# An attention pair with four layer norms on one core: scale and shift of norm 1 moved into W1 and b1, norms 1 and 3 moved to ScalarE, order laid anew

## The chip, the core and the metric

The kernel runs on one core of one Trainium2 chip. Five engines work side by side, each with its own queue in program order: TensorE (PE; its weight loads are shown as PEld), VectorE (DVE), ScalarE (ACT), GpSimd (POOL) and SyncE (SP), which here only issues DMAs. The metric is the device time of one execution in microseconds.

## The reference

32 graphs of 512 nodes with 256 features pass through two attention layers, each with its own adjacency mask, and through four layer norms:

```python
# layer 0
x  = x0 + attention(x0, Wqkv, allowed) @ Wo.T + bo
x  = layernorm(x) * ln1_g + ln1_b                     # norm 1
ff = relu(x @ W1.T + b1) @ W2.T + b2
x  = layernorm(x + ff) * ln2_g + ln2_b                # norm 2
x  = layernorm(x0 + x)                                # norm 3
# layer 1
x  = layernorm(x + attention(x, Wq, Wk, Wv, adj) @ Wo.T + bo)   # norm 4
```

8 heads of 32, W1 from 256 to 1024; everything is float32. `allowed` is adj or its transpose or the diagonal.

## The kernel before

**Tiling.** A graph's 512 nodes are 4 row blocks of 128 partitions (NQ = 4); the 256 features are 2 blocks (ND = 2). Transposed activations (xT, qT, kT) have features on partitions.

**Stages of a graph.** They are small methods of class Graph, each of which issues a few instructions:
- `scores(layer, k)`: for a group of 4 heads and a key block (k = 0 to 7) 4 products with 32 rows of the array each, into psS (four PSUM banks, one buffer), and one exp of ScalarE into p (L340, L344). `masked(layer, k)`: VectorE multiplies p by the mask (L349).
- `product(k)`: 4 products with 32 columns of the array each into psA (L357); products 3 and 7 are followed by a copy to cT on ScalarE (L367). `sums` adds p over keys with a matrix of ones (L397); `pair` adds two p by a GpSimd DMA (L372), `fold` on VectorE (L376), so that `sums` runs once for a head group. `divide` transposes, inverts and multiplies into cT on VectorE (L409 to L416).
- `project` multiplies cT by Wo (psO). `out0`, `out1`, `out2` add the residual on VectorE and take statistics (y L444, st L425, mv L426); `root(n, a, b)` makes 1/sqrt(variance + eps) of the row blocks a to b on GpSimd in two instructions (L431, L432).
- `norm1`, `norm2` call `affine`: two VectorE instructions for each row block (L439, L440). Norm 2 puts the block of x, to which ln2_b has been added, in the place of the shift, so that it adds the residual for norm 3 in the same step. `norm3` is one VectorE instruction (L513). `norm4` is one ScalarE activation (L527), with the bias from `offset` (-mean/std, VectorE, L522).
- `transpose` turns x1 or x2 with TensorE and copies it to xT on ScalarE. `hidden(h, f)` multiplies by W1 and applies relu with b1 on ScalarE (psH L476, hT L484); `mlp` multiplies by W2 (psF L497); `query_key`, `value` are the other projections.
- For later graphs the first transpose is done by DMA: `flip` and `sort` (SP queue) and `join` (two ScalarE copies, L286). `load`, `again` load x twice (x and x1); `cast` and `entries` bring the adjacency, `masks` (VectorE) makes the two masks from it.
- `residual`, `residual1`, `residual2` add rows to x1, x, x1 and x2 by GpSimd DMAs that accumulate (`add_row`, L169). `once` and `once1` (bias rows bov from bv and Wo, TensorE psB L163 and VectorE) do something for graph 0 alone.

**PSUM.** psS takes four banks, psA one, and three buffers in turn (`ps_d`) hold all other results, so that a late reader of one of them holds up the third allocation after it.

**Order.** The order within each engine's queue is written out by hand in three lists of calls: `opening(a, b, c, d)` starts the first graphs, `period(a, b, c, d, e)` is repeated 29 times, and `closing(a, b, c)` ends the last ones. In a period, a to e are five successive graphs: c passes through layer 0's attention in the first half, b through the second half of its MLP and layer 1, a through its last projection and norm 4, d through its first projections. A period begins with c.scores(0, 0). Every engine works through its own calls of the list in order; waits between engines come from the data. Ahead of the opening the SP queue issues the loads: x of graph 0, Wqkv and its biases, the adjacency of graph 0 once it has been cast, Wo and bo of layer 0, x of graph 1, then all other weights in the order of their declaration, layer 1's Wo and bo last.

The general path for extreme inputs at the end of the kernel is not taken in these runs.

Of the kernel before, what the change touches and what calls it, by code (L numbers as in the profile page):

```python
# [9 lines left out]
F32 = mybir.dt.float32  # L10
# [17 lines left out]
def kernel(ctx: ExitStack, tc: tile.TileContext, t: dict, out: bass.AP):  # L28
# [77 lines left out]
    g1, be1 = spread("L0_gnn_ln1_g"), spread("L0_gnn_ln1_b")  # L106
    g2, be2 = spread("L0_gnn_ln2_g"), spread("L0_gnn_ln2_b")
# [11 lines left out]
    bov = [const.tile([P, D], F32, name=f"bov_{layer}") for layer in range(2)]  # L119

# [29 lines left out]
    def plain(pools: ExitStack):  # L150
# [16 lines left out]

        def add_row(dst, row):
            nc.gpsimd.dma_start(out=dst, in_=row[:, None, :].to_broadcast([P, NQ, D]), accum_op=ALU.add)  # L169
# [7 lines left out]
        class Graph:  # L177


            def __init__(self, b):  # L180
                self.b = b
                self.mv, self.rs, self.pf, self.total = {}, {}, {}, {}
# [45 lines left out]
            def once(self):  # L228

                if self.b == 0:  # L230
                    value_bias(0)

# [231 lines left out]
            def norm1(self, i):  # L464
                self.affine(self.x1[:, i, :], self.y.pop(i), g1, be1, 1, i)
# [20 lines left out]
            def residual1(self):  # L486
                add_row(self.x1, b2)
                self.tile("x2", [NQ, D])
# [22 lines left out]
            def norm3(self, i):  # L511
                mean, rs = self.mean(3, i), self.rs[3][:, i, :]
                nc.vector.tensor_scalar(self.x2[:, i, :], self.y.pop(i), mean, rs, ALU.subtract, ALU.mult)  # L513
# [4 lines left out]
            def offset(self, a, b):  # L518

                if a == 0:  # L520
                    self.ms = small.tile([P, NQ, 1], F32, tag="ms", name=f"ms_{self.b}", bufs=2)
                nc.vector.scalar_tensor_tensor(  # L522
                    self.ms[:, a:b, :], self.mv[4][:, a:b, 0:1], -1.0, self.rs[4][:, a:b, :], ALU.mult, ALU.mult
                )

            def norm4(self, i):
                nc.scalar.activation(  # L527
                    self.x2[:, i, :], self.y.pop(i), AF.Identity, bias=self.ms[:, i, :], scale=self.rs[4][:, i, :]
                )
# [7 lines left out]
        def period(a, b, c, d, e):  # L537
# [3 lines left out]
            c.scores(0, 0)  # L541
            a.fold(3, 6, 7)
            b.hidden(1, 0)
            b.hidden(1, 2)
            c.scores(0, 1)
            c.masked(0, 0)
            b.hidden(1, 4)
            b.hidden(1, 6)
            c.masked(0, 1)
            a.fold(3, 3, 4)  # L550
            c.once()
            c.scores(0, 2)
            c.masked(0, 2)
            b.mlp(3)
            b.out2(3)
            a.sums(3, 1, first=True, last=True)
            a.product(7)
            c.scores(0, 3)
            c.product(0)
            b.mlp(2)  # L560
            c.residual()
            a.divide(1)
            b.root(2, 3, 4)
            a.project(1, 0)
            c.scores(0, 4)
            b.transpose(b.x2, 0)
            b.norm2(3)
            c.masked(0, 3)
            c.pair(0)
            b.out2(2)  # L570
            b.root(3, 3, 4)
            b.root(2, 2, 3)
            b.norm3(3)
            a.out1(0)
            a.project(1, 1)
            b.norm2(2)
            c.scores(0, 5)
            c.product(1)
            b.root(3, 2, 3)
            c.product(2)  # L580
            c.product(3)
            a.out1(1)
            c.masked(0, 4)
            b.norm3(2)
            c.scores(0, 7)
            c.masked(0, 5)
            b.transpose(b.x2, 1)
            b.query_key(1, 1, 0, 0)
            c.product(4)
            a.out1(3)  # L590
            a.out1(2)
            c.pair(2)
            a.root(4, 0, 2)
            c.pair(4)
            c.scores(0, 6)
            c.masked(0, 7)
            a.offset(0, 2)
            b.query_key(1, 0, 0, 0)
            c.masked(0, 6)
            c.fold(2, 2, 0)  # L600
            b.query_key(1, 1, 0, 1)
            a.norm4(0)
            a.norm4(1)
            b.query_key(1, 0, 0, 1)
# [4 lines left out]
            c.product(5)  # L609
            c.product(6)  # L610
            a.root(4, 2, 4)
            a.offset(2, 4)
            c.product(7)
            c.sums(2, 0, first=True, last=True)
            b.scores(1, 2)
            b.query_key(1, 0, 1)
            d.entries()
            c.fold(3, 3, 4)
            c.divide(0)
            d.load()  # L620
            d.flip(0, 0)
            d.sort(0, 0)
            d.again()
            d.flip(0, 1)
            c.sums(3, 1, first=True, last=True)
            b.masked(1, 2)
            b.scores(1, 1)
            c.divide(1)
            e.cast()
            b.residual2()  # L630
            b.value(1, 0)
            b.masked(1, 0)
            a.norm4(3)
            a.norm4(2)
            b.value(1, 1)
            c.once1()
            b.masked(1, 1)
            b.scores(1, 5)
            c.project(0, 0)
            c.project(0, 1)  # L640
            b.scores(1, 3)
            c.out0(0)
            c.out0(1)
            c.root(1, 0, 2)
            c.norm1(0)
            c.norm1(1)
            b.product(0)
            b.product(1)
            b.product(2)
            d.join(0, 0)  # L650
            c.out0(3)
            c.out0(2)
            b.scores(1, 7)
            d.sort(0, 1)
            c.transpose(c.x1, 0)
            a.store()
            d.value(0, 0)
            b.scores(1, 6)
# [750 lines left out]
```

## Time and profile before

| What | Value |
|---|---|
| median of 3 runs | 3093.13 us (3093.06 to 3094.09) |
| span of the profiled execution | 3093.4 us |
| instructions in it | 44239 |
| one of the middle periods | 94.8 us |
| DMA | 406.5 MB, mean 131 GB/s |
| mean granted TensorE clock | 0.996 |

A busy share is the part of the span in which an engine has an instruction running. The ends of matmuls are modelled, so starts are safer to read than durations. In a row of instructions, what stands in square brackets is the idle time of the engine before it, and who ended it. A row of a group has the busy time in us, the mean of one in ns, and after the second bar the idle time ahead of its instructions. The 40 digits are slices of 77 us, in tenths.

### The profile page before, as it was taken

What the parts mean: (1) busy time and instruction counts of PE and PEld (TensorE: products, weight loads), DVE (VectorE), ACT (ScalarE), POOL (GpSimd) and SP (SyncE); (2) the same over time, 40 slices, a digit from 0 to 9 for tenths busy, and PEclk for the clock granted to TensorE, in tenths of its full rate; (3) what the DMA queues carried; (4) which work ended last, traced back from release to release, by engine and by line L of the source; (5) the groups of instructions that cost most, each with busy time, mean ns of one, the idle gap of its engine ahead of it and who ended that gap; (6) DMA issues with size and microseconds to landing.
All of it is one profiled execution on the core that took longest, in us unless ns stands there. A gap on an engine that the chain in (4) does not pass through costs nothing. (4 is left out here: it accounts for less than half of the span.)

```text
span 3093.4 us, 44239 instructions
## 1 busy us (share of the span) xinstructions
PE 3053.5 (99%) x17218; PEld 1729.8 (56%) x17218; DVE 2647.5 (86%) x3458; ACT 1707.7 (55%) x1983; POOL 1039.0 (34%) x1254
## 2 busy tenths in 40 slices
PE   6999999999999999999999999999999999999998
PEld 2656555555555555555655555555556555555554
DVE  4798898888898888988888988889888889888887
ACT  4455655555565556655555655556555655555554
POOL 1232334332343323333333333233333334332332
PEclk8999999999999999999999999999999999999999
DMA  8676776666676666776676766668666777666542
GB/s 191 134 135 118 140 144 139 123 130 130 137 151 123 133 125 135 147 139 126 123 136 137 147 120 133 123 137 154 131 132 115 141 143 140 124 129 126 116 89 63
DMA packets 341064, 406.54 MB, mean 131 GB/s; under 512 B 149616, under 2 KB 315632, under 8 KB 316144
## 3 DMA queue, kind: packets, MB, share of 16 engines
q0 software_dynamic: 95824, 282.09, 50.8%
q1 hardware_dynamic: 245024, 121.56, 15.9%
q8 instruction: 137, 2.24, 0.3%
q14 instruction: 79, 0.65, 0.1%
HBM read 89.01 MB, written 33.55 MB: 40 GB/s over the span
## 5 line engine op out<-in xcount | busy, mean ns | idle before, releaser
L344 ACT ACTIVATE p<-psS 128x2048 f32<-128x2048 f32 x512 | 962.3, 1880 | 652.7 <-PE psS L340 647.1
L349 DVE TENSOR_TENSOR p<-p,m 128x2048 f32<-128x2048 f32 x512 | 1155.1, 2278 | 30.6 <-ACT p L344 30.6
L431 POOL TENSOR_SCALAR rs<-mv 128x2 f32<-128x2 f32 (+1 forms) x320 | 321.7, 1005 | 936.0 <-DVE mv L426 934.0
L340 PE MATMUL psS<-qT,kT 32*128 32x512 f32 x4096 | 585.6, 641 | 7.9 <-ACT p L344 6.0
L357 PE MATMUL psA<-p,v 128*32 128x512 f32 x4096 | 491.9, 598 | 0.7 <-ACT cT L367 0.7
L497 PE MATMUL psF<-w_L_gnn_W,hT 128*128 128x256 f32 x2048 | 469.0, 382 | 0.0
L476 PE MATMUL psH<-xT,w_L_gnn_W 128*128 128x256 f32 x2048 | 467.4, 384 | 0.0
L497 PEld LDWEIGHTS psF<-w_L_gnn_W,hT 128*128 128x128 f32 x2048 | 383.7, 190 | 124.9 <-issue 77.7
L476 PEld LDWEIGHTS psH<-xT,w_L_gnn_W 128*128 128x128 f32 x2048 | 381.4, 190 | 118.3 <-issue 44.8
L376 DVE TENSOR_TENSOR p<-p,p 128x2048 f32<-128x2048 f32 x189 | 429.0, 2285 | 2.2 <-DMA p<-p 1.9
L340 PEld LDWEIGHTS psS<-qT,kT 32*128 32x128 f32 x4096 | 160.3, 183 | 305.4 <-issue 114.4
L432 POOL TENSOR_TENSOR rs<-rs,neg_half 128x2 f32<-128x2 f32 (+1 forms) x320 | 304.2, 951 | 26.8
L357 PEld LDWEIGHTS psA<-p,v 128*32 128x32 f32 x4096 | 110.0, 109 | 315.6 <-issue 234.5
L484 ACT ACTIVATE hT<-psH,c_L_gnn_b 128x256 f32<-128x256 f32 x512 | 215.2, 472 | 122.9 <-PE psH L476 119.6
L412 POOL TENSOR_TENSOR total<-total,sT 128x16 f32<-128x16 f32 x128 | 28.5, 223 | 731.2 <-DVE sT L409 731.2
L327 PE MATMUL psQK_None<-xT,w_L_gnn_Wqkv 128*128 128x512 f32 x512 | 239.1, 600 | 4.2 <-DMA w_L_gnn_Wqkv<-in_L_gnn_Wqkv_dram 2.4
L456 PE MATMUL psO<-w_L_gnn_Wo,cT 128*128 128x256 f32 x1024 | 241.1, 383 | 0.9 <-DVE cT L416 0.9
L372 POOL DMA_DIRECT2D p<-p x189 | 186.9, 991 | 142.4 <-PE psA L357 109.3
L367 ACT COPY cT<-psA 128x512 f32<-128x512 f32 x128 | 75.0, 586 | 278.5 <-PE psA L357 278.5
L444 DVE TENSOR_TENSOR y<-psF,x 128x256 f32<-128x256 f32 x128 | 53.7, 420 | 196.1 <-PE psF L497 189.6
L456 PEld LDWEIGHTS psO<-w_L_gnn_Wo,cT 128*128 128x128 f32 x1024 | 189.2, 190 | 51.9 <-DVE cT L416 22.2
L425 DVE BATCH_NORM_STATS2 st<-y 128x6 f32<-128x256 f32 x384 | 164.2, 428 | 13.1
(68 smaller groups left out, 2936.3 us busy)
## 6 DMA issues: line engine op xcount, KB each, us to landing
p<-p POOLq DMA_DIRECT2D x189, 1024.0 KB, 7.6
x<-in_x_dram SPq DMA_DIRECT2D x64, 512.0 KB, 5.2
x<-bov POOLq DMA_DIRECT2D x64, 512.0 KB, 9.1
code<-in_adj_dram POOLq DMA_DIRECT2D x32, 512.0 KB, 6.7
m<-code SPq DMA_DIRECT2D x32, 512.0 KB, 5.6
x<-s_L_gnn_ln_b POOLq DMA_DIRECT2D x32, 512.0 KB, 10.4
x<-s_L_gnn_b POOLq DMA_DIRECT2D x32, 512.0 KB, 5.4
out_dram<-x SPq DMA_DIRECT2D x32, 512.0 KB, 9.4
```

The lines of the kernel that those rows point to most:

```text
L327: nc.tensor.matmul(ps, w[:, i, c * P : (c + 1) * P], self.xT[:, i, at], start=(i == 0), stop=(i == ND - 1))
L340: nc.tensor.matmul(s[:, j, :], self.kT[at, hg, kc * P : (kc + 1) * P], self.qT[at, hg, :], start=True, stop=True)
L344: nc.scalar.activation(p, s, AF.Exp, scale=SCALE)
L349: nc.vector.tensor_tensor(p, p, m[:, k % NQ, None, :].to_broadcast([P, HPC, N]), ALU.mult)
L357: nc.tensor.matmul(self.acc[hg][j * HD : (j + 1) * HD, :], self.v[:, kc, h * HD : (h + 1) * HD], self.p[k][:, j, :], start=(kc == 0), stop ...
L376: nc.vector.tensor_tensor(self.p[dst], self.p[a], self.p[b], ALU.add)
L431: nc.gpsimd.tensor_scalar(rs, self.mv[n][:, a:b, 1:2], EPS, None, ALU.add)
L432: nc.gpsimd.tensor_tensor(rs, rs, neg_half[:, a:b, None], ALU.pow)
L456: nc.tensor.matmul(ps[:, j, :], self.cT[:, k, at], wo[layer][:, k, :], start=(k == 0), stop=(k == ND - 1))
L476: nc.tensor.matmul(ps[:, j, :], w1[:, c, at], self.xT[:, c, h * 2 * P : (h + 1) * 2 * P], start=(c == 0), stop=(c == ND - 1),)
L484: nc.scalar.activation(self.hT[h][:, f + j, :], ps[:, j, :], AF.Relu, bias=b1[:, f + j : f + j + 1])
L497: nc.tensor.matmul(ps, self.hT[h][:, f, j * P : (j + 1) * P], w2[:, f, :], start=(f == 0), stop=(f == NF - 1))
```

## The change

1. Norm 1 writes (y - mean)/std without scale and shift; `fold_norm1`, once for graph 0, multiplies W1's rows by ln1_g in place and adds W1 times ln1_b to b1, so that `hidden` is unchanged. For the residual, `residual1` multiplies x1 by ln1_g on VectorE (after the transposes have read it) and then adds the row ln1_b + b2 (row12) by the same GpSimd DMA as before.
2. Norms 1 and 3 are applied by ScalarE as norm 4 was (`shifted`), with a bias from `offset` for each.
3. The three lists are new. For norms 1 and 3 they have five more `offset` calls in a period. The load section is the same, with two more columns (ln1_g, ln1_b) among the later weights.

```diff
+    g1_c, be1_c = column("L0_gnn_ln1_g"), column("L0_gnn_ln1_b")
...
+    row12 = const.tile([P, D], F32, name="row12")
...
+        def fold_norm1():
+            ps = ps_d.tile([P, NF], F32, tag="d", name="psW_0")
+            for f in range(NF):
+                for c in range(ND):
+                    nc.tensor.matmul(
+                        ps[:, f : f + 1],
+                        w1[:, c, f * P : (f + 1) * P],
+                        be1_c[:, c : c + 1],
+                        start=(c == 0),
+                        stop=(c == ND - 1),
+                    )
+            nc.vector.tensor_tensor(b1, b1, ps, ALU.add)
+            for c in range(ND):
+                nc.vector.tensor_scalar(w1[:, c, :], w1[:, c, :], g1_c[:, c : c + 1], None, ALU.mult)
+            nc.vector.tensor_tensor(row12, be1, b2, ALU.add)
...
+            def once2(self):
+                if self.b == 0:
+                    fold_norm1()
...
             def norm1(self, i):
-                self.affine(self.x1[:, i, :], self.y.pop(i), g1, be1, 1, i)
+
+                self.shifted(1, self.x1, i)
...
             def residual1(self):
-                add_row(self.x1, b2)
+                nc.vector.tensor_tensor(self.x1, self.x1, g1[:, None, :].to_broadcast([P, NQ, D]), ALU.mult)
+                add_row(self.x1, row12)
                 self.tile("x2", [NQ, D])
...
             def norm3(self, i):
-                mean, rs = self.mean(3, i), self.rs[3][:, i, :]
-                nc.vector.tensor_scalar(self.x2[:, i, :], self.y.pop(i), mean, rs, ALU.subtract, ALU.mult)
+                self.shifted(3, self.x2, i)
...
+            def shifted(self, n, dst, i):
+                bias, scale = self.ms[n][:, i, :], self.rs[n][:, i, :]
+                nc.scalar.activation(dst[:, i, :], self.y.pop(i), AF.Identity, bias=bias, scale=scale)
```

The new list of a period, several calls to a line (`sums` without its flags):

```
c.scores(0, 0); b.hidden(1, 0); b.hidden(1, 4); a.fold(3, 6, 7); c.once(); c.scores(0, 1); b.hidden(1, 2);
b.hidden(1, 6); c.masked(0, 0); a.fold(3, 3, 4); c.masked(0, 1); a.sums(3, 1); a.product(7); c.scores(0, 3);
e.cast(); a.divide(1); c.residual(); c.masked(0, 3); b.mlp(3); b.out2(3); b.root(2, 3, 4); b.norm2(3);
c.scores(0, 4); b.mlp(2); c.masked(0, 4); c.scores(0, 2); c.product(0); b.out2(2); a.project(1, 0);
b.root(3, 3, 4); b.root(2, 2, 3); b.offset(3, 3, 4); c.masked(0, 2); c.once2(); c.scores(0, 6); b.norm2(2);
b.transpose(b.x2, 0); c.pair(0); b.root(3, 2, 3); a.out1(0); b.offset(3, 2, 3); a.project(1, 1); a.out1(1);
c.scores(0, 5); a.out1(3); c.masked(0, 5); c.product(1); a.out1(2); b.norm3(3); b.norm3(2); c.product(2);
c.product(3); c.scores(0, 7); c.product(4); c.product(5); b.transpose(b.x2, 1); b.query_key(1, 0, 0, 0);
b.query_key(1, 1, 0, 0); b.query_key(1, 0, 0, 1); c.masked(0, 6); a.root(4, 0, 2); c.pair(2);
a.offset(4, 0, 2); c.masked(0, 7); c.pair(4); c.fold(2, 2, 0); b.query_key(1, 1, 1); b.scores(1, 0);
c.fold(3, 6, 7); a.norm4(0); c.fold(3, 3, 4); a.root(4, 2, 4); c.product(6); c.sums(2, 0); c.product(7);
c.divide(0); b.scores(1, 1); b.query_key(1, 1, 0, 1); b.value(1, 0); c.sums(3, 1); c.divide(1); b.masked(1, 1);
a.norm4(1); b.scores(1, 3); b.query_key(1, 0, 1); c.project(0, 0); b.scores(1, 2); c.project(0, 1); c.out0(0);
c.out0(1); a.offset(4, 2, 4); b.residual2(); c.root(1, 0, 2); c.offset(1, 0, 2); b.masked(1, 0); c.norm1(1);
c.norm1(0); b.value(1, 1); b.masked(1, 2); a.norm4(3); c.transpose(c.x1, 0); b.scores(1, 4); a.norm4(2);
b.product(0); d.again(); d.flip(0, 0); c.out0(3); b.pair(0); d.load(); d.sort(0, 0); c.out0(2); d.entries();
d.flip(0, 1); b.masked(1, 3); b.product(1); b.product(2); d.sort(0, 1); a.store(); d.join(0, 0);
b.scores(1, 7); c.root(1, 2, 4); b.pair(2); c.offset(1, 2, 4); c.once1(); c.norm1(3); b.masked(1, 4);
c.hidden(0, 0); c.norm1(2); c.hidden(0, 2); c.hidden(0, 4); b.scores(1, 6); c.transpose(c.x1, 1);
c.hidden(0, 6); b.scores(1, 5); d.join(0, 1); d.value(0, 0); c.mlp(0); b.masked(1, 7); d.masks();
c.residual1(); d.query_key(0, 1, 0); c.mlp(1); b.masked(1, 6); b.masked(1, 5); b.fold(2, 2, 0); c.out2(0);
c.out2(1); d.query_key(0, 0, 0); d.query_key(0, 1, 1); d.query_key(0, 0, 1); d.value(0, 1); c.root(2, 0, 2);
b.product(3); b.sums(2, 0); b.product(4); b.pair(4); c.norm2(0); c.norm2(1); b.divide(0); c.root(3, 0, 2);
c.offset(3, 0, 2); b.product(5); b.product(6); c.norm3(1); c.norm3(0);
```

The new opening up to graph 0's first transpose of x1:

```
a.flip(0, 0); a.join(0, 0); a.join(0, 1); a.once(); a.query_key(0, 0, 0); a.query_key(0, 1, 0); a.value(0, 0);
a.masks(); a.scores(0, 0); a.query_key(0, 1, 1); a.masked(0, 0); a.scores(0, 3); a.value(0, 1); a.sort(0, 0);
a.scores(0, 1); a.query_key(0, 0, 1); a.scores(0, 2); a.masked(0, 1); a.masked(0, 2); a.masked(0, 3);
a.product(0); a.scores(0, 4); a.product(1); a.masked(0, 4); a.product(2); a.scores(0, 5); a.masked(0, 5);
a.product(3); a.scores(0, 6); a.pair(0); a.pair(2); a.flip(0, 1); b.flip(0, 0); a.product(4); a.pair(4);
b.sort(0, 0); a.masked(0, 6); b.cast(); b.flip(0, 1); a.fold(2, 2, 0); a.scores(0, 7); b.sort(0, 1);
a.product(5); b.join(0, 0); a.masked(0, 7); b.join(0, 1); b.value(0, 0); a.sort(0, 1); a.product(6);
a.product(7); a.sums(2, 0); a.fold(3, 6, 7); a.fold(3, 3, 4); b.entries(); a.residual(); b.residual();
a.divide(0); a.sums(3, 1); b.query_key(0, 0, 0); a.divide(1); b.query_key(0, 0, 1); a.once2();
b.query_key(0, 1, 0); a.project(0, 0); b.scores(0, 0); a.out0(0); a.out0(1); a.root(1, 0, 2);
a.offset(1, 0, 2); b.query_key(0, 1, 1); a.norm1(1); a.norm1(0); a.project(0, 1); a.out0(3); a.out0(2);
b.masks(); a.root(1, 2, 4); c.cast(); b.scores(0, 5); b.masked(0, 0); a.offset(1, 2, 4); a.transpose(a.x1, 0);
...
```

The new closing from c.mlp(0) to the middle of the last attention:

```
...
c.mlp(0); c.mlp(1); b.fold(2, 2, 0); b.masked(1, 5); b.masked(1, 6); c.hidden(1, 0); b.fold(3, 6, 7);
c.out2(0); c.out2(1); b.pair(4); c.root(2, 0, 2); c.norm2(0); b.fold(3, 3, 4); c.norm2(1); c.hidden(1, 4);
c.hidden(1, 6); c.hidden(1, 2); b.sums(2, 0); c.mlp(2); b.divide(0); c.root(3, 0, 2); c.out2(2);
c.offset(3, 0, 2); c.root(2, 2, 3); c.mlp(3); c.norm3(0); c.norm3(1); c.norm2(2); c.out2(3); c.root(2, 3, 4);
c.root(3, 2, 3); c.norm2(3); c.offset(3, 2, 3); c.root(3, 3, 4); c.once1(); b.product(5); b.product(6);
c.transpose(c.x2, 0); c.offset(3, 3, 4); b.product(7); c.norm3(2); c.norm3(3); c.query_key(1, 1, 0, 0);
b.sums(3, 1); b.divide(1); c.transpose(c.x2, 1); c.query_key(1, 0, 0, 0); c.query_key(1, 0, 0, 1);
c.query_key(1, 1, 0, 1); c.scores(1, 0); c.query_key(1, 1, 1); c.scores(1, 1); b.project(1, 0); c.scores(1, 3);
...
```

## The prediction

> **What bounds the kernel now.** I read the busy table, then TensorE's own timeline, because a busy share says nothing about slack, then the opening, where the only long idle stretches lie.
>
> Busy table and 40 slices of the page:
> ```profile
> PE 3053.5 (99%) x17218; PEld 1729.8 (56%) x17218; DVE 2647.5 (86%) x3458; ACT 1707.7 (55%) x1983; POOL 1039.0 (34%) x1254
> ...
> PE   6999999999999999999999999999999999999998
> ...
> PEclk8999999999999999999999999999999999999999
> ```
> TensorE idles in the first slice, somewhat in the last, and nowhere between. VectorE, which the change relieves, has 14% to spare.
>
> TensorE's timeline in a middle period (start, duration, what):
> ```profile
> 1500.94 3.62 PE L497 MATMUL psF<-w_L_gnn_W,hT 128*128 128x256 f32 x16
> 1504.40 1.88 PE L327 MATMUL psQK_None<-xT,w_L_gnn_Wqkv 128*128 128x512 f32 x4
> ...
> 1511.43 2.78 PE L357 MATMUL psA<-p,v 128*32 128x512 f32 x24
> 1514.14 1.14 PE L340 MATMUL psS<-qT,kT 32*128 32x512 f32 x8
> 1515.21 3.72 PE L476 MATMUL psH<-xT,w_L_gnn_W 128*128 128x256 f32 x16
> 1518.87 1.14 PE L340 MATMUL psS<-qT,kT 32*128 32x512 f32 x8
> ```
> Read starts, not durations: each group begins when the one before has run through. Sixteen full-array ("wide") matmuls of 256 columns take 3.46 us with wide neighbours (1500.94 to 1504.40: 0.216 each), but 3.66 between two score groups. So entering and leaving a wide run costs 0.20. A score group takes 1.07 everywhere. Three products take 2.71: 3 x 0.858 plus 0.14 for entering and leaving a column run (products, sums). Nothing else appears: the middle is a fixed sequence of matmuls without waits.
>
> From these prices a period is: 16 score groups x 1.071 = 17.14; 20 products and sums x 0.858 = 17.16; 256 wide units (hidden 64, mlp 64, query_key 64, project 32, value 32; each fp32 product is two records) x 0.2158 = 55.24; 16 transposes x 0.109 = 1.74; 13 wide runs x 0.198 = 2.57; 8 column runs x 0.138 = 1.10; less 0.048 for each of 4 wide runs that begin with a transpose (0.19). Sum 94.77. Measured: the period that opens at 1514.14 ends at 1608.93, 94.79. TensorE sets the pace, and only fewer runs or fewer waits at the two ends can shorten the program.
>
> The opening (all engines):
> ```profile
> 15.03 0.50 SPq L1190 DMA_DIRECT2D w_L_gnn_Wo<-in_L_gnn_Wo_dram  x1
> ...
> 16.53 1.14 PE L340 MATMUL psS<-qT,kT 32*128 32x512 f32 x8 [0.78 <-ACT kT L330]
> ...
> 45.72 2.04 PE L163 MATMUL psB<-w_L_gnn_Wo,c_L_gnn_bv 128*128 128x256 f32 x4 [10.51 <-DMA w_L_gnn_Wo<-in_L_gnn_Wo_dram]
> ...
> 49.97 0.76 ACT L286 COPY xT<-kT 128x512 uint16<-128x512 uint16 x1 [16.95 <-DMA kT<-v]
> ...
> 53.81 2.09 PE L340 MATMUL psS<-qT,kT 32*128 32x512 f32 x8 [6.04 <-ACT p L344]
> ```
> once1() (the bias row of layer 1) stands in TensorE's queue before its weights are there, and graph 1's join() stands in ScalarE's queue before its DMAs are there, with the next exp behind it: 10.5 and 6.0 us of TensorE lost. The first period starts at 186.9; the opening's matmuls at the prices above sum to 151.1, so about 36 us are lost there. The closing (from 2937.4) loses 3.5 before the last matmul, and 10 after it.
>
> **What the skill says.** "Perfetto Trace Analysis", opening note: matmul busy time is a bad measure, as matmuls are pipelined. Hence the starts above. "TensorEngine Tiling (Array Packing)", Key Properties: a change of tiling mode drains TensorE; the trace agrees and prices it (3.46 against 3.66). "SBUF — State Buffer", Who interferes with whom: a VectorE instruction with two SBUF inputs blocks a GpSimd one that reads SBUF. The trace agrees: root()'s first half is 0.36 us free, 2.15 beside a mask product:
> ```profile
> 1574.11 0.36 POOL L431 TENSOR_SCALAR rs<-mv 128x2 f32<-128x2 f32 x1 [5.47 <-DVE mv L426]
> ...
> 1578.93 2.15 POOL L431 TENSOR_SCALAR rs<-mv 128x2 f32<-128x2 f32 x1 [2.76 <-DVE mv L426]
> ```
> "TensorE: Matmul & The Clock Gate", What's actually happening: after idling, the array runs at half clock for some microseconds. The trace agrees: eight matmuls at 9.11 take 7.4 us, eight later ones 3.43.
>
> **Part by part.** Durations are means of the groups by shape.
> ```profile
> L439 DVE SCALAR_TENSOR_TENSOR cent<-y,mv,s_L_gnn_ln_g 128x256 f32<-128x256 f32 x256 | 119.3, 466 | 2.5
> ...
> L440 DVE SCALAR_TENSOR_TENSOR x<-cent,rs,s_L_gnn_ln_b 128x256 f32<-128x256 f32 x128 | 62.0, 485 | 35.9 <-POOL rs L432 30.4
> ...
> L513 DVE TENSOR_SCALAR x<-z,mv,rs 128x256 f32<-128x256 f32 x128 | 48.9, 404 | 36.8 <-POOL rs L432 36.8
> ...
> L527 ACT ACTIVATE x<-y,ms,rs 128x256 f32<-128x256 f32 x128 | 70.2, 600 | 9.5 <-DVE ms L522 9.5
> ```
> *VectorE* loses per graph 4 x (0.466 + 0.485) for norm 1 and 4 x 0.404 for norm 3 = 5.4 us. It gains five offsets x 0.15 and one multiplication of x1 by g1, 1024 wide: between 0.69 (cT, 512 wide) and 2.28 (p, 2048), 1.22. Net -3.4 per graph, -110 in all: 86% becomes 82%. *ScalarE* gains 8 x 0.55 = 4.4 per graph, 55% to 60%. Both lie beside a full TensorE: worth nothing by themselves.
>
> *The period's order.* Counting runs in the new list: wide runs 13 (hidden pair, hidden pair, mlp 3, mlp 2, project 0, transpose and project 1, transpose and query_keys, query_key and value, query_key and project, project and value and transpose, three hiddens, transpose and hidden, the long one from d.value(0, 0)), column runs 8. Same counts, but c.transpose(c.x1, 0) no longer begins a run: +0.048. Floor 94.82, x29 periods = +1.4 us.
>
> *Waits that the order adds.* (a) Norm 1's chain is longer and its window shorter. From the end of c.project(0, 0): two out0 2.04, their last mv starts at 2.05; 1.48 from there to the instruction that waits for root (1573.83 to 1575.31); offset 0.15 and hand-over 0.05; two activations, 0.50 and 0.57; to TensorE about 0.05: 4.8. TensorE fills that with scores(1, 2) 1.07, project(0, 1) 1.83 and value(1, 1) 1.73 = 4.63 before c.transpose(c.x1, 0). Wait 0.2 per period, bounds 0 and 0.35. Behind it queue all wide matmuls. Before, b.product(0..2) and another score group lay in that gap. (b) c.fold(3, 3, 4) waits for pair(4). Pairs are 1 MB POOL DMAs: two issued at 1544.32 and 1548.70 landed 7.2 and 8.4 later, so 5.6 apart. Now product(4) follows product(3) after one score group: pair(2) at about 31.5 of the period lands at 38.6, pair(4) at 44.2. Then VectorE has fold 2.20, divide(0) 2.5, divide(1) 2.6: 51.5, against c.project(0, 0) due at 51.3. Bounds 0 and 0.35; I take 0.1, since a pair issued close behind may land sooner. (c) offset stands in VectorE's queue behind root; with masks following it, VectorE idles 1 us where root was blocked, but the two places (before b.masked(1, 0), b.masked(1, 4)) leave the mask products in time by my sums (S(1, 5) due at 71.86, its psum free at about 71.7). 0. Together 0.3 x 29 = +8.7.
>
> *residual1*: the multiplication precedes the POOL DMA of row12. The product ends at about 75, landing takes 5.4 (median of the b2 row), so 81; out2(0), behind three long VectorE instructions, comes at 81.5. 0. The SP queue has d.again and d.flip first and entries() later; flip waits for c.product(7) (43.5), sort's DMAs land near 54, join is due at 62. 0.
>
> *The opening.* a.once() now stands before the first query_key, and its Wo lands at 19.6 (issued 15.03). First scores: 19.7 + 1.8 (four psB) + 6 (eight at half clock, then full) + value 1.8 = 29 instead of 16.5: +12.5. Against that once1 is late and join stands behind scores(0, 7): -16.6 and some clock warm-up. Eight scores at 3.13 (exp-bound, as 16.53, 19.68, 22.81 before) end at 52; then waits for join (2.6) and fold(3, 3, 4) (3). fold_norm1 on TensorE: 16 products of one column, two passes, 32 records, between 0.109 (a transpose) and 0.216 each: 3.5 to 6.9, I take 6.1 (weight load 0.19). Its VectorE part (two scalings of w1, bias, row12: 3 us) hides beside the next query_key. Laying both lists side by side up to the first norm 1: about +3.3, bounds -3 and +7.
>
> *The closing*: wide runs 20 to 25 = +1.0 and transposes -0.1; a norm 3 chain of 6 us in a window of 5.5 before c.transpose(c.x2, 1): +0.5. Sum +1.4, bounds -1 and +5.
>
> Sum against the profiled span, 3093.4: 3093.4 + 1.4 + 8.7 + 3.3 + 1.4 = 3108.2. The other runs shown, 3093.06 to 3094.09, lie around that span.
>
> **Rivals.**
> *Floor*: neither chain binds, 3093.4 + 1.4 + 3.3 + 1.4 = 3099.5. For it: the margins are 0.1 to 0.2 us, my error.
> *Opening pays* (the other side): fold_norm1 runs at 0.11 per record (-2.6) and join and fold find their DMAs landed (-5.6), no chain binds: 3091. It decides at the first graph's scores(0, 7): if product(5) to sums(3, 1) run without a gap, it holds; with the closing's 3.5 us of waits also gone, 3086 or less. Against: SP's load queue still ends at 41.5.
> *A new wait per period of 1 us or more*: VectorE's stand behind a blocked root() reaches exp and so a score group, or join() meets DMAs that start later. 29 x 1 on top: 3137. For it: root at 2.15 and more beside mask products; against: 15 us of VectorE's period are free.
>
> **Numbers.** Both chains (one at least): 0.54, 3108, own range 3101 to 3118. Floor 0.16. Opening pays 0.16. New wait 0.14. The range 3089 to 3129 leaves out half of the last and the end of the third. No change (within 0.2%, about what a measurement of this kernel can tell) is 3086.9 to 3099.3: half of *opening pays*, near half of *floor*, a little of the first: 0.19; faster 0.11 (half of *opening pays*, some of the closing); slower 0.70.
>
> **What would show it.** Right: period starts 95.1 apart, a wait of psT for ScalarE's x1 and of psO for cT in the list of waits, first psS near 29. Wrong: periods of 94.8 (no chain binds), a first psS before 25, or 32 psW records under 4 us.

## The result: slower, and by more than forecast

| | before | after |
|---|---|---|
| median of the runs, us | 3093.55 (4 runs, 3093.06 to 3094.09) | 3134.83 (4 runs, 3132.3 to 3139.34) |
| profiled span, us | 3093.4 | 3130.5 |
| ratio of the times | | 1.0135, 95% interval 1.0117 to 1.0153 |
| start of the first period, us | 186.89 | 192.49 |
| 29 periods, us: sum (mean, shortest, longest) | 2750.52 (94.845, 94.78, 95.78) | 2781.01 (95.897, 95.01, 97.52) |
| rest (last period and closing), us | 156.0 | 157.0 |

The direction was forecast, the size was not: 3134.8 lies above the range of 3089 to 3129. Between the two profiled spans 37.1 us were lost: 5.6 in the opening, 30.5 in the periods, 1.0 at the end.

The page of the kernel after: busy table, TensorE's 40 slices and its granted clock.
```profile
PE 3070.0 (98%) x17250; PEld 1731.0 (55%) x17250; DVE 2566.1 (82%) x3270; ACT 1828.2 (58%) x2239; POOL 940.1 (30%) x1254
...
PE   6999999999999999999999999999999999999998
...
PEclk9999999999999999999999999999999999999999
```
VectorE fell from 86% to 82%, as worked out, ScalarE rose from 55% to 58% (60% was worked out), and the middle still reads 9 in every slice. A loss of 1 us in 95 is below what a digit can show. The groups, by shape, after:
```profile
L399 DVE TENSOR_TENSOR p<-p,p 128x2048 f32<-128x2048 f32 x189 | 430.0, 2288 | 41.3 <-DMA p<-p 36.3 <-PE psQK_None L350 2.7 <-issue 0.2
...
L552 ACT ACTIVATE x<-y,ms,rs 128x256 f32<-128x256 f32 x256 | 148.8, 595 | 62.9 <-DVE ms L546 57.1 <-issue 5.8
...
L552 ACT ACTIVATE x<-z,ms,rs 128x256 f32<-128x256 f32 x128 | 69.8, 592 | 139.6 <-DVE ms L546 139.6
...
L511 DVE TENSOR_TENSOR x<-x,s_L_gnn_ln_g 128x1024 f32<-128x1024 f32 x32 | 39.0, 1219 | 10.5 <-PE psT L321 10.5
```
Norms 1 and 4 (y) and 3 (z) now have ScalarE's line, and the multiplication by g1 takes 1.22 us, the estimate. The line that matters is the first. fold() is untouched by the change, and its duration is the same (2.29 us), but the idle time in front of it for a pair's transfer is 36.3 us, where the kernel before had 1.9:
```profile
L376 DVE TENSOR_TENSOR p<-p,p 128x2048 f32<-128x2048 f32 x189 | 429.0, 2285 | 2.2 <-DMA p<-p 1.9
```
The list of waits of the kernel after (who, for whom: sum, times, longest) says who passes that on:
```profile
DVE ms L546 <- POOL rs L455: 67.2, 66, 1.5
...
DVE p L399 <- DMA p<-p: 36.3, 41, 3.0
...
PE psB L166 <- DMA s_L_gnn_bo<-in_L_gnn_bo_dram: 12.7, 1, 12.7
...
PE psR L420 <- DVE p L399: 10.9, 10, 2.8
...
PE psR L420 <- DVE sT L432: 5.9, 5, 1.7
...
PE psT L321 <- ACT x L552: 4.4, 15, 0.4
```
VectorE does wait for root in front of its offsets (first line), but of TensorE's waits only the last line, 4.4 us, can lead there. TensorE waits in sums() (psR) for the fold, and for what VectorE does behind the fold. One bad period on three engines (POOL issues the pair, VectorE folds, TensorE sums; this period opens at 1535.29):
```profile
1569.66 0.85 POOL L395 DMA_DIRECT2D p<-p  x1 [2.01 <-DVE st L448]
...
1574.20 4.49 DVE L399 TENSOR_TENSOR p<-p,p 128x2048 f32<-128x2048 f32 x2
...
1580.84 1.89 PE L333 MATMUL psV<-w_L_gnn_Wv,xT 128*128 128x256 f32 x8
...
1581.45 2.29 DVE L399 TENSOR_TENSOR p<-p,p 128x2048 f32<-128x2048 f32 x1 [2.76 <-DMA p<-p]
...
1584.42 1.06 PE L420 MATMUL psR<-p,ones 128*32 128x512 f32 x8 [1.69 <-DVE sT L432]
...
1593.38 1.89 PE L333 MATMUL psV<-w_L_gnn_Wv,xT 128*128 128x256 f32 x8
1595.63 0.66 PE L321 MATMUL psT<-ident,x 128*128 128x128 f32 x4 [0.36 <-ACT x L552]
```
pair(4), issued at 1569.66, lands at 1581.35, 11.7 us later. VectorE has finished the other two folds at 1578.7 and stands for 2.8 us; fold(3, 3, 4) ends at 1583.74. sums(3, 1) starts at 1584.42, 3.58 us after value(1, 0) instead of 1.83. What it waits for last is the "sT" that its row names: the first transpose of divide(0). That instruction stands behind the fold on VectorE and reads the result of sums(2, 0), whose PSUM buffer sums(3, 1), the third allocation after it, takes over. So the late pair reaches TensorE through VectorE's queue and a buffer.

In 15 of the 29 periods pair(4) takes 9.1 to 9.4 us, mostly from 34.4 to 43.5 of the period, and neither sum waits. sums(2, 0) waits in seven periods, where pair(2) took 8.3 us or more instead of 7.1, and sums(3, 1) in five others, where pair(4) took 10.6 to 11.7. These twelve are the periods that are 1.2 us or more above the shortest.

What holds up a pair can be read from the DMA queues (packets, MB, share of the 16 DMA engines). From the issue of pair(4) to its landing, first in the bad period above (1569.7 to 1581.3), then in a quick one (1763.9 to 1773.0):
```profile
q0 software_dynamic: 240, 1.70, 73.1%
...
q8 instruction: 1, 0.02, 0.5%
...
p<-p POOLq DMA_DIRECT2D x1, 1024.0 KB, 11.7
```
```profile
q0 software_dynamic: 240, 1.70, 92.8%
...
p<-p POOLq DMA_DIRECT2D x1, 1024.0 KB, 9.1
```
Queue 8, by its name the fetching of instructions, moves 138 packets of 16 KB in the whole run. A pair ends with sixteen packets of 4 bytes. In the quick period all sixteen are through by 43.2 us of the period; in the bad one fifteen are through by 43.1 and the last comes at 44.5, right behind the instruction packet, which ran from 43.6 to 44.5. In eleven of the twelve long periods such a packet starts between 37.4 and 43.7 us, in the twelfth at 32.3; in the other 17 none starts between 33.2 and 43.2. The fetches fall elsewhere in each period, but much alike in each run: eleven of the twelve are 1.2 us or more above the shortest in runs 3 and 6 below, too. So the lateness is no chance from run to run. No run moves these fetches; this is a reading of the traces and not a test.

The step from one group of matmuls to the next, start to start, averaged over 29 periods and set against the shortest step at the same place, gives the loss by place: sums(2, 0) 0.28 us, sums(3, 1) 0.22, inside project(0, 0) 0.10, the transposes of x1 0.18, and a.sums(3, 1) 0.11 for b.pair(4). On top, the step to the transposes of x1 never falls below 0.34, where 0.22 is the step without a wait (run 6 below): 0.13 in every period.

TensorE in the opening:
```profile
19.48 2.07 PE L166 MATMUL psB<-w_L_gnn_Wo,c_L_gnn_bqkv 128*128 128x256 f32 x4 [12.71 <-DMA s_L_gnn_bo<-in_L_gnn_bo_dram]
...
28.55 1.14 PE L363 MATMUL psS<-qT,kT 32*128 32x512 f32 x8
...
55.10 2.95 PE L333 MATMUL psV<-w_L_gnn_Wqkv,xT 128*128 128x256 f32 x8 [2.26 <-ACT xT L309]
...
65.28 1.07 PE L420 MATMUL psR<-p,ones 128*32 128x512 f32 x8 [2.80 <-DVE p L399]
```
a.once() costs what was forecast: first scores at 28.55 against 29. The new opening's matmuls, with the 3.5 us of fold_norm1, sum to about 154 us at the prediction's prices, those of the old one to 151.1; so TensorE loses about 38 us here instead of about 36.

### The profile page after: what moved, and what is told of

It is laid out like the page before. It is cut to its first block, busy times and chain, and to the rows that moved or that the text cites. A ratio compares the mean times of both kernels' runs of the same rounds, so it can differ in the third digit from the quotient of the medians.

```text
span 3130.5 us, 44346 instructions
## 1 busy us (share of the span) xinstructions
PE 3070.0 (98%) x17250; PEld 1731.0 (55%) x17250; DVE 2566.1 (82%) x3270; ACT 1828.2 (58%) x2239; POOL 940.1 (30%) x1254
## 3 DMA queue, kind: packets, MB, share of 16 engines
q1 hardware_dynamic: 245568, 121.57, 16.5%
## 5 line engine op out<-in xcount | busy, mean ns | idle before, releaser
L380 PE MATMUL psA<-p,v 128*32 128x512 f32 x4096 | 499.5, 598 | 1.9 <-DVE p L372 1.0
L454 POOL TENSOR_SCALAR rs<-mv 128x2 f32<-128x2 f32 (+1 forms) x320 | 258.4, 808 | 727.0 <-DVE mv L449 601.9
L399 DVE TENSOR_TENSOR p<-p,p 128x2048 f32<-128x2048 f32 x189 | 430.0, 2288 | 41.3 <-DMA p<-p 36.3
L395 POOL DMA_DIRECT2D p<-p x189 | 173.1, 916 | 476.8 <-PE psA L380 367.4
L455 POOL TENSOR_TENSOR rs<-rs,neg_half 128x2 f32<-128x2 f32 (+1 forms) x320 | 274.0, 856 | 26.7
L479 PE MATMUL psO<-w_L_gnn_Wo,cT 128*128 128x256 f32 x1024 | 251.6, 388 | 1.4 <-DVE cT L439 0.9
L435 POOL TENSOR_TENSOR total<-total,sT 128x16 f32<-128x16 f32 x128 | 38.5, 301 | 655.8 <-DVE sT L432 653.4
L508 ACT ACTIVATE hT<-psH,c_L_gnn_b 128x256 f32<-128x256 f32 x512 | 206.9, 470 | 45.0 <-PE psH L500 44.4
L552 ACT ACTIVATE x<-y,ms,rs 128x256 f32<-128x256 f32 x256 | 148.8, 595 | 62.9 <-DVE ms L546 57.1
L432 DVE STREAM_TRANSPOSE sT<-psR 128x512 f32<-128x512 f32 x128 | 91.2, 713 | 112.3 <-PE psR L420 109.5
```

Of the source, the lines that this page charges most:

```text
L380: nc.tensor.matmul(self.acc[hg][j * HD : (j + 1) * HD, :], self.v[:, kc, h * HD : (h + 1) * HD], self.p[k][:, j, :], start=(kc == 0), stop ...
L399: nc.vector.tensor_tensor(self.p[dst], self.p[a], self.p[b], ALU.add)
L454: nc.gpsimd.tensor_scalar(rs, self.mv[n][:, a:b, 1:2], EPS, None, ALU.add)
L455: nc.gpsimd.tensor_tensor(rs, rs, neg_half[:, a:b, None], ALU.pow)
L479: nc.tensor.matmul(ps[:, j, :], self.cT[:, k, at], wo[layer][:, k, :], start=(k == 0), stop=(k == ND - 1))
L508: nc.scalar.activation(self.hT[h][:, f + j, :], ps[:, j, :], AF.Relu, bias=b1[:, f + j : f + j + 1])
```

## The experiments

Theory at the start: the new order is the cause, not the moved operations. VectorE reaches its folds just when the pairs usually land, so that each late landing stops TensorE. Rivals: the moved norms, offsets and the multiplication cost the time wherever they stand; or e.cast(), whose place moved by half a period, makes the pairs land late. In all runs the kernel before took 3094.1 to 3094.8 us (medians).

**1. New operations, old order.** The changed kernel with the three lists of the kernel before, an offset ahead of the first norm that needs it, and once2() in the opening:
```diff
             c.root(1, 0, 2)
+            c.offset(1, 0, 2)
             c.norm1(0)
             c.norm1(1)
```


> All new operations (norms 1 and 3 on ScalarE, offsets, folded weights, multiplication by g1) in the order of the kernel before. Theory (the order is the cause): periods stay at 94.8 and only the opening's 3.5 us of psW records is added, 3094 to 3101 us. Rival (the moved norms, the offsets or the multiplication cost it wherever they stand): 3120 us or more, with periods of 95.9.

Measured: 3149.76 us (3145.14 to 3152.32), ratio 1.0177 [1.016, 1.0194]. My theory, as stated, fell. The periods take 95.95 us on average, and unlike those of the changed kernel nearly all take the same 95.8: a constant loss, in three places: 0.25 us ahead of scores(0, 1), 0.20 ahead of transpose(b.x2, 1), 0.56 ahead of d.value(0, 0). TensorE's waits:
```profile
PE psS L363 <- ACT p L367: 14.7, 31, 6.0
...
PE psV L333 <- ACT xT L309: 9.4, 29, 0.7
...
PE psT L321 <- ACT x L552: 8.8, 6, 2.5
...
DVE p L399 <- DMA p<-p: 3.3, 4, 1.5
```
The folds don't wait here (last line). ScalarE does the delaying; its timeline at the second line's place:
```profile
1611.56 1.09 ACT L552 ACTIVATE x<-y,ms,rs 128x256 f32<-128x256 f32 x2 [0.30 <-DVE ms L546]
1612.55 1.38 ACT L309 COPY xT<-kT 128x512 uint16<-128x512 uint16 x2
```
The two activations of norm 1, held up by their offset, stand ahead of the copies of d.join(0, 0), and d.value(0, 0) waits for these. So the moved norms do cost time in the old order, through what is queued behind them on ScalarE, an engine that is 58% busy. The opening lost another 18 us (first period at 204.81).

**2. Old operations, new order.** The kernel before with the three new lists, without the offsets of norms 1 and 3 and without once2().


> The operations of the kernel before (norms 1 and 3 on VectorE, nothing folded) in the new order. Theory: the folds still stand right behind the landings of their pairs and VectorE now has 3.4 us more work per period, part of it ahead of them, so 3130 to 3150 us, with folds waiting for pairs as in the changed kernel. Rival (moved operations): about 3093 us, at most 3100.

Measured: 3241.01 us (3235.78 to 3242.09), ratio 1.0474 [1.0457, 1.0492]; periods of 99.2. More than the theory allowed, and for another reason:
```profile
PE psT L298 <- DVE x L440: 75.4, 30, 2.7
...
DVE p L376 <- DMA p<-p: 23.8, 46, 2.6
...
PE psT L298 <- DVE x L513: 11.3, 30, 1.9
```
The new list has b.masked(1, 0) between root and norm 1. With norm 1 on VectorE, its instructions stand behind that mask product of 2.28 us, and the transposes wait 2.5 us in each period. Runs 1 and 2 together: neither half of the change can be judged alone. The order was laid for ScalarE norms, but it wins back next to nothing of what these lose in the old one: the 29 periods sum to 2782.5 us in run 1 and to 2781.0 in the changed kernel. Of the 16.5 us between the two profiles 12.3 lie in the opening and 2.8 in the closing.

**3. Old opening, the rest new.**


> The changed kernel with the opening's order of the kernel before (new operations, the weights folded behind the first graph's second divide). Theory: the period carries the loss, so the first period starts about 3 us sooner (190) and the program takes 3128 to 3136 us. Rival (the opening carries a good part): under 3120 us.

Measured: 3149.85 us (3149.17 to 3151.11), ratio 1.018 [1.0163, 1.0197]. The first period starts at 204.70 instead of 192.49; I expected 190. With the new operations the old opening is 12 us worse than the new one, so the expected gain has the wrong sign. The period is indeed not helped: mean 96.05. The first takes 101.3: there TensorE waits 3.4 us at scores(0, 1), because ScalarE stands 8.9 us before norm 3 until its offset comes, which is queued behind a divide() on VectorE.

**4. The suspected wait taken away.** Two lines less in the period:
```diff
-            c.pair(2)
...
-            c.pair(4)
```


> The changed kernel without the two pair transfers for p2 and p4 of layer 0 in the period (the sums then lack p3 and p5). Theory (folds stand right behind landings of varying time): sums(2, 0), sums(3, 1) and project(0, 0) don't wait any more, periods near 95.0 to 95.2, 3105 to 3112 us. Rival (moved norms, offsets, or VectorE's own load): the folds begin no sooner than VectorE's masks let them, 3128 us or more.

Measured: 3112.76 us (3110.01 to 3115.76), ratio 1.0058 [1.0041, 1.0075], 22 us less than the changed kernel, as the theory said. Mean period 95.09, and 24 of 29 take 95.01. In the profiles the 29 periods lose 23.4 us against the changed kernel, while the first one starts 5.0 us later, although the opening is the same. The waits now:
```profile
DVE p L399 <- DMA p<-p: 9.6, 10, 3.0
...
PE psR L420 <- DVE p L399: 4.4, 4, 2.8
```
The four losses at and behind the two folds (0.28 + 0.22 + 0.10 + 0.18 = 0.78 us, times 29 is 22.6) are gone; those 0.18 at the transposes only passed on the delay of the folds. What stays is 95.01 in place of the floor's 94.82, and a.sums(3, 1).

**5. The cast at its old place.**
```diff
-            e.cast()
...
             c.divide(1)
+            e.cast()
```


> The changed kernel with e.cast() of the period back at its old place, behind c.divide(1). Theory (the folds stand right behind their pairs, whatever else the DMA engines do): the waits at sums(2, 0) and sums(3, 1) stay, 3130 to 3138 us. Rival (the cast, which now starts 7 us behind b.pair(4) and 23 us ahead of c.pair(0), is what makes pairs land late): 3118 us or less.

Measured: 3169.28, 3202.82, 3227.57 and 3287.5 us (median 3215.19); ratio of the two lower ones 1.0296 [1.0233, 1.0358]. The rival is out: pair(4) still takes 9.1 to 11.7 us, and 10.5 or more in the same eleven periods. And something worse comes on top: single periods take up to 134 us. The waits of the run profiled (span 3285.7, the longest of the four):
```profile
ACT xT L309 <- DMA kT<-v: 181.8, 33, 37.8
...
PE psQK_None L350 <- ACT xT L309: 134.0, 16, 37.3
```
At its old place the cast now meets bov's addition and the four transposing loads of d's mask. In the 134 us period, the transposing load of d.flip(0, 1), issued behind these, took 45.0 us; in the changed kernel's periods of 95.0 us it takes 3.1 to 4.1. The join and d.query_key waited for it. So the cast's new place is no part of the loss at the folds of c, and the new order needs it away from these loads. What it does to b.pair(4) is seen in run 10.

**6. Norm 1's first two rows back on VectorE** (y less mean, times rs, ahead of the mask; no offset for them; in the opening and the closing likewise).
```diff
             c.root(1, 0, 2)
-            c.offset(1, 0, 2)
-            b.masked(1, 0)
             c.norm1(1)
             c.norm1(0)
+            b.masked(1, 0)
```


> The changed kernel with norm 1 of the first two row blocks applied by VectorE in one instruction each, behind root and ahead of the mask product that followed the offset. Theory (norm 1's chain through offset and ScalarE costs 0.13 us in every period at the least): the step from value(1, 1) to the transposes falls to 0.22 and the shortest period from 95.01 to 94.82; the pairs' waits stay, so 3126 to 3133 us. Rival (the chain costs nothing, the transposes wait for something else): shortest period still 95.01, 3132 to 3138 us.

Measured: 3149.63 us (3148.85 to 3151.38), ratio 1.0179 [1.0162, 1.0196]. The transposes' wait vanished, as the theory said (the step is 0.22), but the shortest period rose to 95.58:
```profile
PE psA L380 <- DVE p L372: 17.7, 47, 0.7
```
b.product(0) and b.product(2) now wait 0.37 and 0.55 us for b.masked(1, 0) and b.masked(1, 2), which stand some 0.65 us later on VectorE (two instructions of 0.40 in place of one of 0.15). I had priced the chain that I shortened and not the instruction queued behind it. The chain's 0.13 us is real, but VectorE is the wrong place to win it back.

**7. More lead for the pairs, nothing left out.**
```diff
-            c.product(1)
+            c.product(2)
...
-            c.product(2)
+            c.product(1)
+            c.pair(2)
...
             c.product(6)
+            c.product(7)
             c.sums(2, 0, first=True, last=True)
-            c.product(7)
```


> The changed kernel with pair(2) about 0.8 us sooner (product(2) ahead of product(1), pair(2) ahead of root) and sums(2, 0) one product later; nothing is left out. Theory (0.5 us of slack against a landing that varies by 2 is the cause): sums(2, 0) never waits, sums(3, 1) seldom, mean period 95.1 to 95.3, 3112 to 3120 us. Rival (the late pair(4) alone counts, which this moves little): 3126 us or more.

Measured: 3117.02 us (3116.55 to 3121.18), ratio 1.0077 [1.006, 1.0094]: 18 us won by a pair issued 0.9 us sooner and sums one product later. sums(2, 0) never waits and sums(3, 1) hardly (0.004 us on average instead of 0.22); the mean period is 95.33. With run 4 this shows the cause of about half of the 41 us lost from both sides: take the transfers away, or give them slack.

**8. The kernel before with another opening.** The flips and sorts of graph 1 ahead of the loads of layer 1's weights, the joins behind the eighth scores, the bias row of layer 1 behind project(0, 1).


> The kernel before with another opening alone: graph 1's flips and sorts go to the queue ahead of the loads of layer 1's weights, its joins stand behind the eighth scores, the bias row of layer 1 behind project(0, 1). Theory (TensorE's 16.6 us of waits in the opening are the order of two queues): the first period starts 12 to 18 us sooner, all periods 94.8, 3075 to 3082 us. Rival (the loads are bound by the DMA engines, the wait only moves): 3088 us or more.

Measured: twelve runs from 3092.65 to 3139.66 us, median 3113.47, ratio without the two highest 1.0058 [1.0027, 1.0088]. The theory fell: even the lowest three, at 3092.7 to 3095.5, only equal the kernel before. In the run profiled the first period starts at 201.65, 15 us later than before: value(0, 0) of graph 1 waits 26.5 us for the join, whose transposing loads run beside the pairs.

**9. The old order of the period, mended for ScalarE.** TensorE's order is the old one; five places on ScalarE and VectorE differ. New opening, old closing.
```diff
             c.scores(0, 0)
+            b.norm3(1)
+            b.norm3(0)
...
+            a.out1(1)
+            b.offset(3, 2, 3)
+            b.norm3(2)
             c.product(2)
             c.product(3)
...
             c.root(1, 0, 2)
+            d.join(0, 0)
             c.offset(1, 0, 2)
```


> All new operations in the period's old order with five of ScalarE's and VectorE's places mended: norm3 of rows 0 and 1 behind the next period's first exp, offset and norm3(2) ahead of a mask and of cT's copy, d.join(0, 0) ahead of norm 1 (TensorE's order is the old one, and so are the pairs); opening of the changed kernel, closing in its old order. Theory (the moved norms cost only where a ScalarE instruction that TensorE needs soon is queued behind them): the 1.0 us that each period lost with the plain old order is gone, periods 94.8 to 94.9, 3098 to 3106 us. Rival (ScalarE's extra work or the longer norm chains cost it in any place): periods of 95.3 or more, 3115 us or more.

Measured: 3115.83 us (3114.47 to 3119.73), ratio 1.0074 [1.0058, 1.0089]. Theory and rival share this: the time is in the rival's range, the periods, all at 95.19 but one, lie between the two. Two of the three losses of run 1 are gone; 0.40 us is left where transpose(c.x1, 0) waits for the second activation of norm 1, now behind the join's copies.

**10. Run 7 with e.cast() 12 us later, clear of b.pair(4).**


> The changed kernel with the earlier pairs and the later sums as in the run before, and e.cast() some 12 us later, clear of b.pair(4) ahead of it and of c.pair(0) behind it. Theory: b.pair(4) lands in 7 to 8 us always, a.sums(3, 1) at 9.1 of the period waits no more, mean period 95.1 to 95.2, 3110 to 3116 us. Rival (the cast has no part in b.pair(4)'s late landings): as without the move, 3116 to 3121 us.

Measured: 3120.21 us (3115.41 to 3121.46), ratio 1.0085 [1.007, 1.01]. Nothing won against run 7. In the profile a.sums(3, 1) lost 0.04 us per period instead of 0.12 (2.3 us in 29 periods if the move did it), which is below the spread of these runs. The landings themselves are clear: b.pair(4) takes 8.0 us at the median in run 7 and 7.0 here, as it does in run 5, where the cast is away too. So the cast does delay b.pair(4), by 1.0 us; what this costs the program is too small to be seen in its time.

**11. The kernel before, two queues of the opening alone.** As run 8, with the loads left in their order.


> The kernel before with the loads left in their order; in the opening only the joins stand behind the eighth scores and the bias row of layer 1 behind project(0, 1). Theory: value(0, 0) can start at 52 instead of 60.7, but query_key needs the second join, whose transfer lands near 61, so 2 to 4 us are won, 3089 to 3092 us. Rival (TensorE idles at one stretch instead of two and runs at the lower clock afterwards): no gain, 3093 to 3096 us.

Measured: 3112.63 us (3109.34 to 3122.84), ratio 1.0056 [1.0043, 1.007]: slower, against both. The opening on POOL and SP in this run:
```profile
41.74 0.85 POOL L372 DMA_DIRECT2D p<-p  x1 [7.70 <-DVE p L349]
42.28 1.65 POOL L169 DMA_DIRECT2D x<-bov  x1
43.05 2.17 POOL L169 DMA_DIRECT2D x<-s_L_gnn_ln_b  x1
43.81 1.96 POOL L204 DMA_DIRECT2D code<-in_adj_dram  x1
44.35 2.76 POOL L169 DMA_DIRECT2D x<-bov  x1
...
44.55 10.11 SPq L256 DMA_TRANSPOSE v<-in_x_dram  x1
...
73.29 2.67 SPq L273 DMA_DIRECT2D kT<-v  x4
```
And in the kernel before:
```profile
42.57 1.97 SPq L256 DMA_TRANSPOSE v<-in_x_dram  x1
...
47.04 2.67 SPq L273 DMA_DIRECT2D kT<-v  x4
...
61.12 0.85 POOL L372 DMA_DIRECT2D p<-p  x1 [27.00 <-PE psA L357]
```
Without the two waits TensorE finished product(4) sooner, pair(4) and five more POOL transfers went out 19 us sooner, and graph 1's flip, issued 2 us later than before, landed 28.7 us after its issue instead of 4.4. The 16.5 us of waits that I had counted as a loss of the kernel before kept these transfers apart.

**12. The join ahead of an exp.** Run 9 with d.join(0, 0) ahead of b.scores(1, 3).


> As the mended old order, with d.join(0, 0) one step sooner, ahead of b.scores(1, 3)'s exp, where ScalarE is idle for 2.8 us and the transfers for the join have landed 11 us before; norm 1 has no copy ahead of it then. Theory (the 0.40 us left in each period are the join's 1.4 us in front of norm 1): periods 94.8, 3102 to 3107 us, what is left being the opening (5.9 us) and the closing (3 us). Rival (norm 1's chain through offset and ScalarE is too long for this place whatever stands before it): periods 95.1 to 95.2, 3113 to 3118 us.

Measured: 3105.42 us (3104.12 to 3109.68), ratio 1.0038 [1.0026, 1.0051]. The theory held: 28 of 29 periods take 94.78, as in the kernel before. The page and the waits of this run:
```profile
PE 3057.6 (98%) x17250; PEld 1734.1 (56%) x17250; DVE 2552.3 (82%) x3270; ACT 1826.6 (59%) x2239; POOL 929.6 (30%) x1254
...
DVE p L399 <- DMA p<-p: 8.7, 9, 2.8
```
With all moved operations in it, VectorE at 82% and ScalarE at 59%, the period costs nothing more and gains nothing. The 10.9 us between this span (3104.3) and that of the kernel before are the opening (first period at 195.63, +8.7) and the closing (+3.5), less 1.3 in the periods' sum. The median of no experiment lies below that of the kernel before.

## Why the prediction was right and wrong, point by point

- **The bound.** Right. TensorE at 98% sets the pace, VectorE's relief (2647 to 2566 us) is worth nothing, and run 12 shows it cleanly: same period with and without the moved norms.
- **The floor**, +1.4 us for a period of 94.82: right as far as it shows. The shortest periods are 95.01, which is this floor and 0.19; 0.13 of it is (a), 0.06 is not located.
- **(a) Norm 1's chain**, 0.2 per period with bounds 0 and 0.35: right. The wait at the transposes is 0.13 at the least, and run 6 removed it there. Its mean of 0.31 holds 0.18 that comes from the folds (run 4).
- **(b) pair(4) to the fold**, 0.1 with bounds 0 and 0.35: this is the step that failed. The mechanism was named, and the ordinary landings were well placed: 38.6 and 44.2 worked out, 38.5 and 43.5 measured. The term was mis-sized, in three ways. First, the landing was taken as one number, 7.2 and 8.4 us, from a single period. Over its 29 periods the kernel before already shows 7.0 to 8.6 for pair(2) and 8.2 to 10.4 for pair(4); in the changed kernel pair(4) takes 9.1 to 11.7. Second, pair(2) was taken only as pair(4)'s predecessor, while fold(2, 2, 0) and sums(2, 0) wait for it themselves, with 0.5 us between the fold's end and the sums where the kernel before had 1.6: that place lost the most (0.28). Third, a late pair(4) was set against c.project(0, 0) alone, while sums(3, 1), behind divide(0)'s first transpose, stops sooner (0.22). Together these places lose 0.78 us per period, 22.6 us in all and 22 us in run 4, in place of 0.1 and 2.9. The wait of a.sums(3, 1) for b.pair(4), 0.11 per period, is not in the prediction at all.
- **(c) Offset behind root**, 0: right in the changed kernel. VectorE stood 67 us there, and TensorE's list shows only 1.0 us of waits for a mask product, in the opening. Run 6 shows how little room there was.
- **residual1**, 0: right in the period; out2 waited for the row twice, 2.0 us in all.
- **SP's queue**, 0: right as far as seen; joins wait only in the opening (9.7 us in two waits).
- **The opening**, +3.3 with bounds -3 and +7: +5.6 in the profiled run, inside the bounds, but one profile says little here. In runs 4, 5, 7 and 10 the same opening lets the first period start between 193.3 and 198.2, +6.4 to +11.3; why it varies is open. First scores 29 against 28.55. The 32 psW records took 3.5 us and not 6.1, each 0.11, the price of a transpose. Of the 7.4 us read for the first eight matmuls at 9.11, 0.78 are a wait for kT; the row itself is 6.65 long, which still fits half the clock. The waits for the join and for fold(3, 3, 4) came as worked out (2.3 and 2.8 us against 2.6 and 3). With psW 2.6 us cheaper than taken, the other terms of the laying side by side were together 4.9 us too low in this run; which of them, the runs don't tell.
- **The closing**, +1.4: +1.0.
- **The rival "a new wait per period of 1 us or more"** had the size (3137 against 3134.8; 1.05 us per period) by luck, for it had the wrong cause: neither a root() that blocks exp nor a join. It should have been the wait of (b), with its spread. **Opening pays** fell by its own test: product(5) to sums(3, 1) of the first graph do not run without a gap (the sums at 65.28 wait 2.8 us for their fold), although fold_norm1 ran at 0.11 per record, as it assumed. **Floor** fell by (a) alone.
- What the list of signs said of "right" came half true: the wait of psT for x1 is in the list and first scores are near 29, but psO for cT is there only once, 0.9 us, as in the kernel before, and the periods lie not 95.1 apart but anywhere from 95.01 to 97.5. That scatter is the sign that a transfer sets the end. One sign of "wrong" appeared: the psW records took under 4 us. It belongs to the opening and not to (b).

What stays open: runs 4 and 7 show what the late landings cost, but that instruction fetches make them late is read from the traces and not tested. Also open are the 0.06 us per period and the opening's spread.

## What to carry to other kernels

When an edit moves the consumer of a transfer, list every consumer and put the slack beside the spread of the landings in the trace, not beside one of them: steps that fit with 0.5 to 0.8 us to spare in the ordinary round made 12 of 29 rounds 1.2 us or more longer, and cost as much as a fixed wait of 0.8. Look also at what else uses the DMA engines in the late rounds, instruction fetches included. Moving work to an engine that is half idle costs what is queued behind it there; find that by asking who waits for the next instruction on the engine. And a wait of the bottleneck can keep two groups of transfers apart: before you take it away, look at what the earlier finish will issue, and what that meets.

## What the runs showed of the hardware

- **A transposing load beside POOL's transfers**: 4.4 us in the kernel before's opening, ahead of most of POOL's transfers; 28.7 beside six of them (run 11); 45.0 beside a cast, an addition and two pairs, and behind the mask's four transposing loads (run 5). The Trainium skill, "DMA: Bandwidth & Descriptors", section Queues, rings and completion order, says that each DMA engine takes turns between its queues packet by packet, which would let a small load through early. That these loads wait nearly until the large transfers have ended is more than I would read from it; what holds them up is not shown here.
- **An instruction fetch beside a pair**: pair(4) takes 10.5 to 11.7 us in eleven periods, in each of which a 16 KB packet of the instruction queue starts while it is on its way (37.4 to 43.7 us of the period), and 9.1 to 9.8 in the 17 in which none starts between 33.2 and 43.2. In the late period read above fifteen of its sixteen closing packets are on time and one comes 1.4 us later.
- **The price of a pair**: the same page's section "Anatomy of one DMA — SWDGE (gpsimd) path" fits 2.0 us and 436 KB per us, an estimate of 4.4 us for 1 MB. The shortest landing seen here, from issue, is 7.0 us (SBUF to SBUF, adding), and two issued 3 us apart land 5.0 apart. The measured number decides.
- A product of a single column (psW) takes 0.109 us in a row of them, half of one with 256 columns.
